# Attention outputs of six batches a layer as seven products added to the residual stream, tokens filled in batch by batch, and statistics of the last layer one a stage

## The chip, the core and the metric

The kernel runs on one core of a Trainium2 chip. Its engines are TensorE (PE, with weight loads as PEld), VectorE (DVE), ScalarE (ACT), GpSimd (POOL) and SyncE (SP), which issues most DMAs. Each works through its own queue in order and waits on semaphores for the others. The metric is the device time of one execution in microseconds (us), a median over runs. All data is float32.

## The reference

Eight batches of 512 tokens of width 512 pass two layers; each has a cross attention to 120 context rows of the batch, and a feed-forward part. LN is a layer norm.

```python
x = x + tanh(g_xattn[0]) * L0_xattn(LN(x), ctx)          # 16 heads of 32
x = x + tanh(g_ffn[0])   * L0_ffn(LN(x))                 # routed in groups of 32 tokens
x = x + tanh(g_xattn[1]) * L1_xattn(LN(x), ctx, mask)    # with biases and a key mask
x = x + tanh(g_ffn[1])   * L1_ffn(LN(x))                 # mixes each token with the one before
# attention: q = x Wq', k = ctx Wk', v = ctx Wv'; out = softmax(q k' / sqrt(32)) v; return out Wo'
```

## The kernel before

The stream `x` stays in SBUF, 32 tiles of 128 tokens, four tiles a batch. `CrossAttention` first projects keys and values (`project_keys`, `project_values`), then runs one stage a tile (`run`, then `tail` for the last tiles). The order on PE is written out by hand in the source; in the loop `run` the order on DVE, ACT and POOL is a planner's and fixed in the built program.

Stage t works on several tiles at once: `scores(t + 1)` makes the scores s of the next tile and emits its softmax, `queries` makes a quarter of the query products of the next batch, `output(t - 1)` multiplies the attention result of the tile before with Wo, `transpose_probs(t)` transposes this tile's probabilities, `transpose_x` transposes a normalised tile of two batches on (xnps to xnT), `after(t, 1)` does routing products in layer 0 (rlps, rxps, pps), and `attend(t)` multiplies probabilities with values (aps, copied to aT). `output` is split: two of its four matmuls stand before `transpose_probs`, two behind; in every fourth stage it is three and one.

The softmax of a tile is, on DVE, a maximum of each half of s (mx, nmx), a subtraction in the first half (L527), a sum (L533) and reciprocals (L506); on ACT eight exponentials of the second half (L517) and one of the first (L528); on POOL a scaling of each half (L507). `transpose_probs` then writes tps, copied to prT by DVE (first half) and ACT (second half).

PSUM has two pools. `p_s` has two places, tag "s", taken in turn by the two halves of s and the two halves of tps (L474, L543). `p_mm` has four places, tag "mm", taken in turn by every other product.

`SevenProducts` computes a 512 x 512 x 512 product in seven quarter products (`p1` to `p7`, each four matmuls of 256 columns, `multiply`) where the plain way takes eight. It needs four sums of quarters on each side (`left_steps`, `right_steps`); queries, keys, gates and values of the last layer use it already. Their sums for queries are made on POOL.

In layer 0, `route_stats` takes a tile's layer norm statistics (DVE, then three small POOL steps, L58 to L61), and `route_norm` writes the tile aside by DMA and normalises it in place on ACT (L714). In layer 1, `stats` only measures; the tiles of the last two batches are measured in `ChannelMix.run`, inside its stages of seven products.

## Time and profile before

| | us |
|---|---|
| median of 3 runs | 1442.75 (1442.69 to 1443.22) |
| profiled execution, own time | 1441.8 |
| its span | 1440.0 |
| layer 0 attention, one batch in the loop | 49.6 |
| layer 1 attention, one batch in the loop | 44.4 |
| PE busy in the span | 1386.5 |
| output products (L598), 512 records | 239.6 busy, 594 ns each |

The span is that of the instructions in the trace; the execution's own time is 1.8 us more. A matmul in float32 shows as two records, a transpose as one; records overlap, so a group's pace is read from starts: eight records of L598, one tile, take 3.44 us start to start, eight of L149 (one of the seven products) 1.72. In a time-ordered view a row has start, length, engine, line, operation, output<-input, and count of merged records; in brackets stands the idle time before it and what ended it. In a view by stretches the columns are length and the busy time of PE, PEld, DVE, ACT, POOL, then granted clock, DMA share and GB/s.

### The profile page before, as it was taken

The page shows a single profiled execution, that of the slowest core. Times are in us where ns is not written, and L with a number is a line of the kernel's source. Part 1 is how long each engine was busy: PE and PEld are TensorE (multiplying, and loading weights), DVE is VectorE, ACT ScalarE, POOL GpSimd, SP SyncE. Part 2 cuts the span into 40 slices and gives each one's busy share as a digit, 9 for nine tenths or more (in the row PEclk, how much of TensorE's full clock was granted, in tenths as well). Part 3 has the DMA queues.
Part 4 walks back from the last instruction along what each step waited for, and adds up shares of the span by engine and source line. Part 5 has one row for each costly group of instructions (what it writes and reads, how often), then busy time and mean ns, then how long its engine had stood idle before and what let it go on. Part 6 is the DMA issues. An engine that isn't in the chain of part 4 may idle for free.

```text
span 1440.0 us, 32567 instructions
## 1 busy us (share of the span) xinstructions
PE 1386.5 (96%) x13728; PEld 1067.2 (74%) x13728; DVE 1022.6 (71%) x1457; ACT 770.6 (54%) x1874; POOL 643.4 (45%) x576
## 2 busy tenths in 40 slices
PE   7999999999999997999999999999998999999997
PEld 3477777777776787888657777777775888888886
DVE  2767767777777776777576777777777677777786
ACT  1246666666666445444225665666566644445543
POOL 0425545545543001555375665666547233343331
PEclk9999999999999999999999999999999999999999
DMA  9200000000001347433301000000000000000001
GB/s 301 104 9 23 24 23 23 24 21 18 24 30 46 126 134 228 120 105 86 117 0 60 2 2 2 1 2 2 2 30 2 1 30 30 30 30 30 30 16 44
DMA packets 44886, 69.46 MB, mean 48 GB/s; under 512 B 2891, under 2 KB 20811, under 8 KB 44739
## 3 DMA queue, kind: packets, MB, share of 16 engines
q1 hardware_dynamic: 44451, 67.37, 14.5%
q8 instruction: 108, 1.77, 0.5%
q14 instruction: 39, 0.32, 0.1%
q10 hardware_dynamic: 288, 0.00, 0.0%
HBM read 50.59 MB, written 16.78 MB: 47 GB/s over the span
## 4 chain that ended last, share of the span: by engine, by line
PE 71%; DVE 15%; ACT 6%; POOL 4%; issue 3%; DMA 1%; POOLq 0%; DVEq 0%; ACTq 0%
PE ops L598 14%; PE qps L149 13%; PE tps L546 6%; PE cps L149 5%; PE aps L581 4%; PE s L489 4%; PE kps L342 4%; PE rps L992 3%; PE vps L361 3%; PE rlps L731 2%; PE l1ps L907 2%; PE ops L1013 2%; DVE rT L972 2%; PE xnps L421 2%; PE gps L880 2%
## 5 line engine op out<-in xcount | busy, mean ns | idle before, releaser
L507 POOL TENSOR_TENSOR pr<-pr,rs 128x960 f32<-128x960 f32 x128 | 229.0, 1792 | 250.6 <-DVE rs L506 229.2
L598 PE MATMUL ops<-wo,aT 128*128 128x512 f32 x512 | 239.6, 594 | 0.7 <-ACT aT L589 0.7
L517 ACT ACTIVATE pr<-s,nmx 128x120 f32<-128x120 f32 x512 | 176.7, 371 | 113.6 <-DVE nmx L514 105.5
L598 PEld LDWEIGHTS ops<-wo,aT 128*128 128x128 f32 x512 | 92.2, 190 | 71.9 <-issue 67.0
L1005 POOL TENSOR_TENSOR r<-r,b 128x1024 f32<-128x1024 f32 x31 | 73.5, 2378 | 144.3 <-ACT r L1004 144.3
L149 PE MATMUL qps<-xnT,wq 128*128 128x256 f32 x512 | 119.6, 381 | 0.0
L546 PEld LDWEIGHTS tps<-ident,pr 128*120 128x120 f32 x864 | 96.8, 138 | 29.5 <-issue 26.2
L525 DVE TENSOR_REDUCE mx<-s 128x8 f32<-128x960 f32 x64 | 73.9, 1155 | 56.7 <-PE s L489 56.7
L517 ACT ACTIVATION_READ_ACCUMULATOR pr<-s,nmx 128x1 f32 x512 | 111.1, 217 | 0.0
L546 PE MATMUL tps<-ident,pr 128*120 128x128 f32 x864 | 104.8, 273 | 2.5 <-ACT pr L517 1.3
L149 PEld LDWEIGHTS qps<-xnT,wq 128*128 128x128 f32 x512 | 95.7, 189 | 15.2 <-issue 1.0
L533 DVE TENSOR_REDUCE sm<-pr 128x8 f32<-128x960 f32 x64 | 73.5, 1149 | 22.1 <-ACT pr L528 22.0
L49 DVE BATCH_NORM_STATS2 bnst<-x 128x6 f32<-128x512 f32 x128 | 86.8, 678 | 1.3
L422 ACT COPY xnT<-xnps 128x512 f32<-128x512 f32 x64 | 38.0, 594 | 82.1 <-PE xnps L421 82.1
L514 DVE TENSOR_REDUCE nmx<-s 128x8 f32<-128x960 f32 x64 | 73.5, 1148 | 5.7 <-PE s L489 5.7
L581 PE MATMUL aps<-prT,v 120*32 120x128 f32 x2048 | 72.3, 276 | 4.7 <-ACT prT L571 2.7
L527 DVE TENSOR_TENSOR pr<-s,mx 128x960 f32<-128x960 f32 x64 | 73.5, 1149 | 0.9
L556 ACT COPY prT<-tps 120x1024 f32<-120x1024 f32 x54 | 55.0, 1018 | 32.6 <-PE tps L546 32.6
L1258 POOL TENSOR_TENSOR x<-x,cv 128x512 f32<-128x512 f32 x28 | 39.7, 1416 | 71.9 <-DVE cv L1255 71.9
L489 PE MATMUL s<-kT,qT 32*128 32x120 f32 x2048 | 71.1, 275 | 0.0
L489 PEld LDWEIGHTS s<-kT,qT 32*128 32x128 f32 x2048 | 65.6, 186 | 6.4 <-issue 6.3
L581 PEld LDWEIGHTS aps<-prT,v 120*32 120x32 f32 x2048 | 53.2, 109 | 18.7 <-issue 8.4
(189 smaller groups left out, 3101.7 us busy)
## 6 DMA issues: line engine op xcount, KB each, us to landing
w<-in_w_dram SPq DMA_DIRECT2D x32, 512.0 KB, 5.0
x<-in_x_dram SPq DMA_DIRECT2D x8, 1024.0 KB, 15.6
aside<-x SPq DMA_DIRECT2D x32, 256.0 KB, 2.0
x<-aside SPq DMA_DIRECT2D x8, 1024.0 KB, 10.2
out_dram<-x SPq DMA_DIRECT2D x14, 512.0 KB, 2.8
ctx<-in_ctx_dram SPq DMA_DIRECT2D x4, 960.0 KB, 11.7
wk<-in_wk_dram SPq DMA_DIRECT2D x3, 1024.0 KB, 11.2
wv<-in_wv_dram SPq DMA_DIRECT2D x3, 1024.0 KB, 6.2
```

The source lines that it names most:

```text
L49: cm.nc.vector.bn_stats(st, cm.x[:, t, :])
L149: self.nc.tensor.matmul(ps[:, m, :], self.a[a][:, k, m * P : (m + 1) * P], self.b[b][:, k, :], start=(k == 0), stop=(k == 1),)
L489: nc.tensor.matmul(s[j // 2][:, j % 2, hc * LK : (hc + 1) * LK], self.qT[b][r : r + 32, hc, toks], self.kT[r : r + 32, hc, keys], start=no ...
L507: nc.gpsimd.tensor_tensor(pr[:, js, :, :], pr[:, js, :, :], rs[:, js, :, :].to_broadcast([P, 2, NC, LK]), ALU.mult,)
L514: nc.vector.tensor_reduce(nmx, sv[1], AX.X, ALU.max, negate=True)
L517: nc.scalar.activation(pr[:, 2 + j, hc, :], sv[1][:, j, hc, :], AF.Exp, bias=nmx[:, j, hc, :], accum_out=sm[:, 2 + j, hc : hc + 1],)
L525: nc.vector.tensor_reduce(mx, sv[0], AX.X, ALU.max)
L527: nc.vector.tensor_tensor(pv, sv[0], mx.to_broadcast([P, 2, NC, LK]), ALU.subtract)
L533: nc.vector.tensor_reduce(sm[:, :2, :], pv, AX.X, ALU.add)
L546: nc.tensor.transpose(ps[:, jj, hc * P : (hc + 1) * P], pr[:, 2 * u + jj, hc, :], self.cm.ident,)
L581: nc.tensor.matmul(aps[32 * j : 32 * j + 32, hc, :], self.v[b // 2][:LK, b % 2, h * HD : (h + 1) * HD], prT[:, j, hc, :], start=True, stop ...
L598: nc.tensor.matmul(ops, self.aT[t][:, c, :], self.wo[:, c, :], start=(c == 0), stop=(c == NC - 1),)
```

## The change

In both layers the outputs of batches 0 to 5 are made by seven products a batch (`SevenAdded`) from aT of four tiles and Wo, in place of four `output` calls. Products are added to `x` with the gate as they come: on DVE from PSUM, and for a sum shared by several quarters (t) through ACT or DVE and then POOL. Wo's four sums are made once a layer on POOL (`wos`), aT's four once a batch on DVE. aT becomes one buffer of four tiles, xnT one buffer; their sums lie in buffers of the coming queries. Tiles of x are now transposed, and queries made, batch by batch: in the last stage of a batch three transposes and two output products, in the first stage of the next one transpose and four output products, then one output product and seven query products in the two stages after. Batches 6 and 7 keep `output`, unsplit. Routing follows two tiles later and catches up in two late stages. In `ChannelMix` two tiles a stage are normalised and transposed, in two stages each; of the last two batches, one tile is measured in each stage of values and keys. The core of the diff:

```diff
@@ -110,7 +110,7 @@
             step(t3, b22, b12, ALU.subtract),
             step(t1, b12, b11, ALU.subtract),
             step(t2, b22, t1, ALU.subtract),
-            step(t4, t2, b21, ALU.subtract),
+            step(t4, *((b21, t2) if negated else (t2, b21)), ALU.subtract),
         ]
 @@ -204,6 +204,51 @@
         self.finish(0, 1, c12)
+class SevenAdded(SevenProducts):
+    def __init__(self, nc, psum, a, b, c, t, gate, order):
+        super().__init__(nc, psum, a, b, c, None, order=order)
+        self.t, self.gate = t, gate
+    def add(self, c, ps):
+        self.nc.vector.scalar_tensor_tensor(c, ps, self.gate, c, ALU.mult, ALU.add)
+    def add_sum(self, *places):
+        for c in places:
+            self.nc.gpsimd.tensor_tensor(c, c, self.t, ALU.add)
+    def p1(self):
+        ps = self.multiply("A11", "B11")
+        self.nc.scalar.activation(self.t, ps, AF.Copy, scale=self.gate)
+        self.add_sum(self.c[0, 0])
+    def p2(self):
+        self.add(self.c[0, 0], self.multiply("A12", "B21"))
+    def p5(self):
+        ps = self.multiply("S1", "T1")
+        self.add(self.c[0, 1], ps)
+        self.add(self.c[1, 1], ps)
+    def p6(self):
+        self.add(self.t, self.multiply("S2", "T2"))
+        self.add_sum(self.c[0, 1])
+    def p7(self):
+        self.add(self.t, self.multiply("S3", "T3"))
+        self.add_sum(self.c[1, 0], self.c[1, 1])
+    def p3(self):
+        self.add(self.c[0, 1], self.multiply("S4", "B22"))
+    def p4(self):
+        self.add(self.c[1, 0], self.multiply("A22", "T4"))
@@ -255,6 +299,10 @@
                 for b in (1, 2):
                     self.stats_of_batch(b)
             self.work = pool("at_work", 2)
+            sums = self.work.tile([P, 4, 2, 256], FP, name="wos", tag="xnT")
+            self.wos = [sums[:, i] for i in range(4)]
+            self.xnT = self.work.tile([P, NC, S + 1], FP, name="xnT")[:, :, :S]
+            self.aT = self.work.tile([P, NC, S], FP, name="aT", bufs=1)
             self.prologue()
...
@@ -377,17 +425,27 @@
         for b in range(3):
             self.project_values(b)
-        for t in range(2 * TB):
+        for t in range(TB):
             self.transpose_x(t)
             self.normalize(t + 2)
             if t < TB - 1:
                 self.project_values(t + 3)
-            elif t < 2 * TB - 1:
-                self.queries(0, t + 1 - TB)
-        rest = self.scores(0)
-        for b in range(B - 2, B):
-            self.project_values(b)
+        self.start_queries(0)
+        self.queries(4)
+        self.project_values(B - 2)
+        self.queries(2)
+        self.project_values(B - 1)
+        self.queries(1)
+        rest = None
+        for t in range(TB, 2 * TB):
+            self.transpose_x(t)
+            if t + 2 < 2 * TB:
+                self.normalize(t + 2)
+            if t == TB:
+                rest = self.scores(0)
         rest()
+        self.start_queries(1)
+        self.sum_output_weights()
...
@@ -432,35 +485,47 @@
             step()
         self.wq7 = SevenProducts.left(w, *sums)
+    def sum_output_weights(self):
+        w, sums = self.wo, self.wos
+        for step in SevenProducts.right_steps(w, *sums, self.nc.gpsimd, negated=True):
+            step()
+        self.wo7 = SevenProducts.right(w, *sums)
+    def quarters_of_queries(self, b):
+        if b not in self.qT:
+            self.qT[b] = self.work.tile([P, NC, S], FP, name="qT")
+        return {(i, j): quarter(self.qT[b], i, j) for i in (0, 1) for j in (0, 1)}
+    def bank(self):
+        return self.p_mm.tile([P, 2, 256], FP, name="qps", tag="mm")
     def start_queries(self, b):
-        xnT = self.xnT[b][:, :, :S]
-        own = self.work.tile([P, 2, 256], FP, name="xns", bufs=1)
-        sums = [quarter(xnT, 0, 1), quarter(xnT, 0, 0), own, quarter(xnT, 1, 0)]
-        engine = self.nc.gpsimd if b > 1 else self.nc.vector
+        nc, xnT = self.nc, self.xnT
+        c = self.quarters_of_queries(b)
+        sums = [quarter(xnT, 0, 1), quarter(xnT, 0, 0), c[1, 0], quarter(xnT, 1, 0)]
+        engine = nc.gpsimd if b > 1 else nc.vector
         steps = SevenProducts.right_steps(xnT, *sums, engine)
         for step in steps[:2]:
             step()
         self.later_sums = steps[2:]
-        self.xn7 = SevenProducts.right(xnT, *sums)
-    def queries(self, b, f):
...
+        self.q7 = SevenProducts(
+            nc, self.bank, self.wq7, SevenProducts.right(xnT, *sums), c,
+            lambda: quarter(xnT, 0, 1),
+            bias=(self.bqk[:, 0, 0:2], self.bmore) if self.biased else None,
+        )
+    def queries(self, n):
+        for _ in range(n):
+            self.q7.next()
+            if self.later_sums:
+                self.later_sums.pop(0)()
     def scores(self, t):
@@ -585,28 +650,41 @@
                     start=True,
                     stop=True,
                 )
-        self.aT[t] = self.work.tile([P, NC, P], FP, name="aT")
-        nc.scalar.copy(self.aT[t], aps)
-    def output(self, t, chunks):
-        nc, x = self.nc, self.cm.x
-        if 0 in chunks:
-            self.ops[t] = self.p_mm.tile([P, D], FP, name="ops", tag="mm")
-        ops = self.ops[t]
-        for c in chunks:
+        nc.scalar.copy(self.aT_of(t), aps)
+    def aT_of(self, t):
+        i = t % TB
+        return self.aT[:, :, i * P : (i + 1) * P]
+    def output(self, t):
+        nc, x, aT = self.nc, self.cm.x, self.aT_of(t)
+        ops = self.p_mm.tile([P, D], FP, name="ops", tag="mm")
+        for c in range(NC):
             nc.tensor.matmul(
-                ops,
-                self.aT[t][:, c, :],
-                self.wo[:, c, :],
-                start=(c == 0),
-                stop=(c == NC - 1),
+                ops, aT[:, c, :], self.wo[:, c, :], start=(c == 0), stop=(c == NC - 1)
             )
...
+        nc.vector.scalar_tensor_tensor(
+            x[:, t, :], ops, self.gate, x[:, t, :], ALU.mult, ALU.add
+        )
+    def start_outputs(self, b):
+        nc, aT = self.nc, self.aT
+        x = self.cm.x[:, b * TB : (b + 1) * TB, :]
+        c = self.quarters_of_queries(b + 2)
+        sums = [quarter(aT, 0, 1), c[0, 0], c[1, 1], c[0, 1]]
+        self.output_sums = SevenProducts.left_steps(aT, *sums, nc.vector)
+        self.o7 = SevenAdded(
+            nc, self.bank, SevenProducts.left(aT, *sums), self.wo7,
+            {(i, j): quarter(x, i, j) for i in (0, 1) for j in (0, 1)}, c[1, 0], self.gate,
+            "1256734",
+        )
     def after(self, t, stage):
@@ -616,31 +694,55 @@
     def run(self):
-        for t in range(-1, NT - TB - 1):
-            if t >= 0:
-                if t + 10 < NT:
-                    self.normalize(t + 10)
-                self.scores(t + 1)()
-            self.queries(*divmod(t + TB + 1, TB))
+        self.after(-1, 1)
+        for t in range(NT - TB - 1):
+            b, i = divmod(t, TB)
+            if i in (1, 2) and b + 2 < B:
+                self.normalize(TB * (b + 2) + i - 1)
+            if i == 1 and b > 0:
+                self.o7.next()
+            self.scores(t + 1)()
+            if i == 0 and b > 0:
+                self.transpose_x(TB * (b + 1) + 3)
+            if i == 3:
+                self.start_outputs(b)
+                self.transpose_x(TB * (b + 2))
+                self.normalize(TB * (b + 2) + 2)
+                self.o7.next()
+                self.transpose_x(TB * (b + 2) + 1)
+                self.normalize(TB * (b + 2) + 3)
+            elif i == 0 and b > 0:
+                self.o7.next(2)
+            elif b > 0 or i < 2:
+                self.queries(2)
             self.after(t, 0)
-            short = t % TB == TB - 2
-            ahead = 3 if short else 2
-            if t > 0:
-                self.output(t - 1, range(ahead))
-            x_ahead = short and not self.masked
-            if x_ahead and t + 9 < NT:
-                self.transpose_x(t + 9)
-            if t >= 0:
-                self.transpose_probs(t)
-            if t > 0:
-                self.output(t - 1, range(ahead, NC))
-            if t + 9 < NT and not x_ahead:
-                self.transpose_x(t + 9)
+            if t - 1 >= NT - 2 * TB:
+                self.output(t - 1)
+            self.transpose_probs(t)
+            if i == 3:
+                self.transpose_x(TB * (b + 2) + 2)
+            elif i == 0:
+                if b > 0:
+                    self.o7.next(2)
+                else:
+                    self.queries(1)
+            elif i == 2:
+                self.queries(2)
+            elif b > 0:
+                self.queries(1)
             self.after(t, 1)
-            if t >= 0:
-                self.attend(t)
+            self.attend(t)
+            if i == 3:
+                for step in self.output_sums:
+                    step()
+                self.o7.next()
+            elif i == 0 and b > 0:
+                self.start_queries(b + 1)
             self.after(t, 2)
     def tail(self):
@@ -753,25 +857,41 @@
             ALU.is_equal,
         )
+    @staticmethod
+    def tiles_ended(s):
+        if s < 24:
+            return [s - 4] if s >= 4 else []
+        return {24: [20, 21], 25: [22, 23, 24]}.get(s, [s - 1])
     def in_slot(self, s, attention, stage):
         last = NT - TB - 1
-        if stage == 2 and 0 <= s - 1:
-            self.route_stats(s - 1)
-        if (stage == 2 and (0 <= s - 1 < last - 1 or s == NT)) or (stage == 3 and s > last):
-            self.route_norm(s - 1 if stage == 2 else s - 2)
-        if stage != (0 if s == NT else 1):
-            return
-        pool = attention.p_mm
+        if stage == 2:
+            for t in self.tiles_ended(s):
+                self.route_stats(t)
+                if t < last - 1 or s == NT:
+                    self.route_norm(t)
+        if stage == 3 and s > last:
+            self.route_norm(s - 2)
         if s == -1:
             self.start()
-        if 0 <= s - 4:
-            self.route_logits(s - 4, pool.tile([P, D], FP, name="rlps", tag="mm"))
-        if 0 <= s - 3:
-            self.route_x(s - 3, pool.tile([P, D], FP, name="rxps", tag="mm"))
-        b = (s - 9) // TB
-        if (s - 9) % TB == 0 and 0 <= b < B - 2:
-            self.route_back(b, pool.tile([P, D], FP, name="pps", tag="mm"))
+        def bank(name):
+            return attention.p_mm.tile([P, D], FP, name=name, tag="mm")
+        if stage == (0 if s == NT else 1) or (stage == 0 and s in (last - 2, last - 1)):
+            t = self.t
+            if 0 <= t - 1:
+                self.route_logits(t - 1, bank("rlps"))
+            if 0 <= t:
+                self.route_x(t, bank("rxps"))
+            self.t += 1
+        if stage == (0 if s == NT else 1):
+            b = 5 if s == 29 else (s - 11) // TB
+            if s == 29 or ((s - 11) % TB == 0 and 0 <= b < B - 3):
+                self.route_back(b, bank("pps"))
...
@@ -1332,10 +1463,9 @@
                 work += sums(b + 1, 1)
             if b + 2 < B:
                 work += calls(self.normalize, *[(TB * (b + 2) + i,) for i in range(TB)])
+            work = self.turns(work)
             if b < TB:
-                t = NT - 2 * TB + 2 * b
-                work += calls(self.at.stats, *[(t + i,) for i in range(2)])
+                work[4].insert(0, lambda t=late + 2 * b: self.at.stats(t))
             self.stage(self.values(b), work)
```

## Prediction

> **What bounds it now.** I read the busy shares first, then the busy time by stretches of one batch, then the time-ordered TensorE rows of a stage with and without output products.
>
> ```profile
> PE 1386.5 (96%) x13728; PEld 1067.2 (74%) x13728; DVE 1022.6 (71%) x1457; ACT 770.6 (54%) x1874; POOL 643.4 (45%) x576
> 264.00:313.60 49.60, 49.60 (x481) 38.18 (x477) 35.42 (x57) 33.23 (x96) 25.34 (x26) 1.00 0.06 23
> 887.50:932.00 44.50, 44.50 (x445) 32.86 (x442) 32.90 (x47) 27.38 (x87) 27.83 (x23) 1.00 0.01 1
> ```
>
> The columns of the stretches are length, then PE, PEld, DVE, ACT, POOL busy. In both attention layers PE is busy all of a batch's 49.6 or 44.4 us, so a removed matmul pays in full only while everything feeding PE stays in time. How much time it has is seen in two stages of layer 0, a usual one and the first (t=0), which has no output products:
>
> ```profile
> 286.55 1.17 PE L489 MATMUL s<-kT,qT 32*128 32x120 f32 x32
> 287.65 1.99 PE L149 MATMUL qps<-xnT,wqs 128*128 128x256 f32 x8
> 289.48 1.89 PE L149 MATMUL qps<-xnT,wq 128*128 128x256 f32 x8
> 291.21 1.88 PE L598 MATMUL ops<-wo,aT 128*128 128x512 f32 x4
> 292.92 1.91 PE L546 MATMUL tps<-ident,pr 128*120 128x128 f32 x16
> ```
>
> ```profile
> 93.86 1.17 PE L489 MATMUL s<-kT,qT 32*128 32x120 f32 x32
> 94.96 1.99 PE L149 MATMUL qps<-xnT,wqs 128*128 128x256 f32 x8
> 96.79 1.89 PE L149 MATMUL qps<-xnT,wq 128*128 128x256 f32 x8
> 99.23 1.06 PE L546 MATMUL tps<-ident,pr 128*120 128x128 f32 x8 [0.56 <-DVE pr L527]
> 100.97 1.09 PE L546 MATMUL tps<-ident,pr 128*120 128x128 f32 x8 [0.67 <-ACT pr L517]
> ```
>
> Scores and probability transposes take turns in the same two PSUM places: tps of tile t overwrites s of tile t+1, its first half once DVE has subtracted the maximum (L527), its second once the eight exponentials (L517) have read. In the usual stage PE has two query products (3.56 us) and half an output (1.72) between s and tps. At t=0 only the queries stand there, and PE stalls.
>
> ```profile
> 287.75 1.16 DVE L525 TENSOR_REDUCE mx<-s 128x8 f32<-128x960 f32 x1 [1.26 <-PE s L489]
> 290.01 0.36 ACT L517 ACTIVATE pr<-s,nmx 128x120 f32<-128x120 f32 x1 [1.66 <-DVE nmx L514]
> 292.71 1.04 ACT L528 ACTIVATE pr<-pr 128x960 f32<-128x960 f32 x1
> ```
>
> From the end of s (287.65) the subtraction ends after 3.4 us (three 1.07 us steps) and the exponentials after 5.06. The second half of tps came at 292.92+0.87: 1.1 us to spare. That spare is the quantity to watch.
>
> **Products.** A 512-column matmul is two records, 0.86 us (3.44 a tile, 13.75 a batch); a 256-column one 0.43, so seven products are 28 x 0.43 = 12.03. Saved: 1.72 a batch, 20.6 for twelve. Everything else on PE is only moved.
>
> **What stands before tps now.** By the order of the changed program, between s and tps: last stage of a batch (call it 3): transpose, product, transpose = 2.7 us; stage 0: transpose and two products = 4.1; stages 1 and 2: two products = 3.56. All under the 4.2 (5.06 less tps's own first half, 0.87) that the second half needs. I walk layer 0 from the end of stage 3's s, each engine in its static order.
>
> Stage 3: tps starts 3.4, second half 5.06, ends 5.9 instead of 4.5. ACT then runs the pv exponential (to 6.05), the new scaled copy, an xnT copy and a normalisation before prT's second half (8.65); the next xnT copy, whose bank attend needs, ends 9.15. Attend ends 10.2, against 7.85 without waits: stall 2.35. Layer 1 has no routing work to cover this: attend would end at 5.97 and ends at 9.65 (third matmul waits for prT): 3.7.
>
> PE then does product 2 (to 11.95) and s (13.05). Stage 0: the four new sums need the last aT copy (10.85); DVE does them and product 2's add before the next maximum. At 0.69 each they end 14.2, while s was ready at 13.05. Subtraction 17.4, exponentials 19.1; PE reached tps at 17.1. Stall 1.2; layer 1, where the sums meet POOL work, 1.75.
>
> Stage 1: after tps (20.0) come products 7 and 3, routing, attend (25.9), product 4 (27.6) and s (28.7). DVE owes seven adds a batch (0.74 each, the four old STTs gone), two output adds and the stats, and starts the maximum 1.1 us late. Layer 1: o4 ends 26.4, s 27.6; DVE adds o4, takes two stats and aggregates (to 28.7), then maximum, negated maximum, subtraction to 31.9; exponentials end 33.6, 6.0 after s where two products and half of tps cover 4.4: stall 1.6. In layer 0 four of L714's normalisations stand together on ACT ahead of these exponentials. They wait for POOL: after the last x additions (26.9) come two query sums (1.1 each, to 29.2), then four chains, each 0.22+0.57+0.27 us from rows L58, L59, L61 and gaps, 5.0 in all: 34.2. The aside DMAs (2.0 us) are done by then. Last normalisation 35.0, q1's copy 35.5, exponentials 38.2, where s ended at 28.7: stall 5.1. Queued behind are q1's copy, DVE's add of it, and PE.
>
> Stage 2: DVE is punctual again, 5.06 against 4.4: 0.7.
>
> Sums: layer 0 9.4 - 1.7 = +7.7 a batch; layer 1 7.75 - 1.7 = +6.0. The sixth window keeps outputs of batch 6 between s and tps in stages 1 and 2 (+3.44), which hides 3.4 + 0.7 = 4.1 of waits in layer 0 and 1.6 + 0.7 = 2.3 in layer 1. So 6 x 7.7 - 4.1 = **+42**, 6 x 6.0 - 2.3 = **+34**.
>
> **First batch.** s(1) follows s(0) with only transposes between, so waits for s(0)'s readers (4.1 stall). Stage 0: batch 1's sums between DVE's maximum steps (row: one such sum took 1.70 before the maximum at t=0), 1.7. Stage 1: 0.7, and attend directly after tps 1.1. Stage 2: nothing before tps, 4.2. That is 11.8 against 4.0 before in layer 0 and about 2 in layer 1: **+18**.
>
> **Other costs.** POOL gets four 1.2 us additions a batch (25.3 + 4.8 = 30 of 57 us busy) and wos (four of 1.27): POOL waits elsewhere, 0; without that cover each would push a probability scaling by 1.2. The copy with the gate equals L161's 0.57 on ACT, counted above. Layer 1's stats in mix.run: gates of four batches stall 1.0 and some 0.3 more behind kT's last add; later batches (no stats) don't. Between 0 and -5.3; I take **-2**, since DVE's total before that add is unchanged. Route tiles two stages later, caught up in two late stages, and the paired mix transposes: PE work conserved, that tail had 4.1 us of waits, bound -3 to +3, 0.
>
> **A rule against a row.** The Trainium skill's "TensorE: Matmul & The Clock Gate" (Part 1) says that an idle window of about 3.4 us halves PE's clock for another. In this trace 1.41 us is the longest mid-run wait I found, with clock 1.00; but after the first 9.35 us the 16 ctps took 3.44 against 1.81 later. By the row of short waits, 0. By the rule five 5.1 us and two 4.2 us stalls would contain a whole window about half the time: 7 x 0.5 x 1.63 = 5.7, an estimate; I take **+4**, ends 0 and 11.
> "GPSIMD Engine Reference" (specifications) says two-input SBUF work on DVE contends with POOL. L107 on DVE took 0.69 where alone, 1.44 at the worst form's mean. Four sums at 0.69 are 2.8 us, contended 5.7. POOL mostly waits then: I take the first; the end is 3 x 12 = 36 more.
>
> **Sum.** 42 + 34 + 18 - 2 + 4 = +96. The profiled execution was 1441.8 (span 1440.0), 0.95 under the median: 1441.8 + 96 = **1538**.
>
> **Rivals.**
> Floor (25%): DVE punctual, ACT not blocked by normalisations. Then stalls are 2.35/3.7, 0.05, 0.7, 0.7, layer 0 +2.1, layer 1 +3.4 a batch: 6 x 5.5 - 2.8 + 18 = +48: 1490. For it: the static order is a planner's, and the statistics may become ready sooner than I walk. Against: t=0's trace shows a DVE sum delaying tps directly.
> Contention (11%): sums at the contended price, clock halved: +96 + 36 = 1574. Against: POOL is mostly waiting at those moments.
> Gain (3%): tps does not wait, saving all of 20.6: 1421. It decides where exponentials end within 4.4 us of s, below 5.06; nothing in the trace does so. Against it: t=0's two waits.
> Losses just cancelling the gain: 1%. Not doing what it says: the order shows 28 matmuls a batch in place of 16, so no chance of its own.
> Main, 60%, own range 1515 to 1560.
>
> **Range.** 1488 to 1566 takes in floor and main, leaving most of contention and gain out. A measurement tells 0.2% (3 us) from no change. Faster 0.03, same 0.01, slower 0.96.
>
> **What would show it.** PE idle before tps released by the exponentials and the subtraction in every stage; in layer 0 largest at stage 1, ending just after four normalisations; batch stretches of about 57 and 50 us; PE busy 20 us less. Wrong if PE stays full in these stretches, or if the exponentials end within 4.4 us of s.

## The result, and the profile after

| | before | after |
|---|---|---|
| median | 1442.72 us (1438.88 to 1443.22) | 1581.62 us (1577.82 to 1585.01) |
| profiled execution, own time | 1441.8 | 1585.0 |
| its span | 1440.0 | 1583.2 |
| mean granted clock of PE | 0.998 | 0.974 |

The ratio is 1.0964, with a 95% interval of 1.0943 to 1.0986: the change costs 139 us. Slower was forecast, 1538 us, with a range to 1566; the measured time lies 15.6 us beyond the upper end.

First the busy shares after the change, then the view by stretches: one batch of layer 0, one of layer 1, and the sixth and last such window of layer 0.

```profile
PE 1421.3 (90%) x14016; PEld 1144.2 (72%) x14016; DVE 1094.4 (69%) x1541; ACT 778.7 (49%) x1886; POOL 720.9 (46%) x632
248.70:309.10 60.40, 52.06 (x504) 44.20 (x500) 40.99 (x64) 33.62 (x96) 30.07 (x30) 0.94 0.05 19
943.30:998.00 54.70, 46.40 (x472) 38.05 (x472) 39.15 (x53) 28.21 (x88) 33.91 (x26) 0.97 0.00 1
429.56:492.83 63.27, 58.85 (x544) 48.16 (x540) 45.26 (x76) 34.58 (x98) 32.18 (x36) 1.00 0.07 26
```

Three things are to be seen. A batch takes 60.4 and 54.7 us in place of 49.6 and 44.4, where about 57 and 50 had been forecast. PE is no longer full: it idles 8.3 us in each of the two batches. And PE is busy 35 us *more* over the whole run, although 20.6 us of matmuls were taken out, while the clock column fell to 0.94 and 0.97. The second fact is the mechanism of the forecast; the third is what it missed.

The view of PE's waits names the mechanism. Before, no row of tps in it came to more than 1.4 us in total; now two such rows are at the top. The columns are the total, the count and the longest.

```profile
PE tps L611 <- ACT pr L582: 51.5, 48, 4.5
PE tps L611 <- DVE pr L592: 34.5, 32, 3.5
PE aps L646 <- ACT prT L621: 13.9, 10, 1.7
```

L582 and L592 are the exponentials and the subtraction (L517 and L527 before), L611 the transposes of the probabilities. So tps does wait for the readers of the next tile's scores, in nearly every stage. The worst stage is the one forecast, stage 1 of layer 0. Here it is in time order on PE:

```profile
277.91 1.17 PE L554 MATMUL s<-kT,qT 32*128 32x120 f32 x32
279.00 3.72 PE L149 MATMUL qps<-xnT,wq 128*128 128x256 f32 x16
283.76 1.06 PE L611 MATMUL tps<-ident,pr 128*120 128x128 f32 x8 [1.03 <-POOL rstd L59]
288.24 1.96 PE L611 MATMUL tps<-ident,pr 128*120 128x128 f32 x8 [3.42 <-ACT pr L582]
289.99 3.48 PE L149 MATMUL qps<-xnT,wqs 128*128 128x256 f32 x8
```

and on ACT, where four normalisations of the routed layer (L818, L714 before) wait for POOL's chains and stand ahead of the exponentials; the last two are these, with a query copy and the first exponential behind them:

```profile
283.26 1.70 ACT L818 ACTIVATE x<-x,nmr,rstd 128x512 f32<-128x512 f32 x2 [0.71 <-POOL nmr L61]
284.86 0.56 ACT L161 COPY qT<-qps 128x512 f32<-128x512 f32 x1
285.33 0.36 ACT L582 ACTIVATE pr<-s,nmx 128x120 f32<-128x120 f32 x1
```

The reader should now compare lengths on PE. Behind the wait, eight transposes take 1.96 us and one product 3.48, where the other stages show 1.09 and 1.89. PE runs at half clock there. The view by stretches says so directly. Taken for PE alone, its columns are length, PE busy, granted clock, DMA share and GB/s:

```profile
282.96:286.37 3.41, 1.06 (x8) 1.00 0.00 0
286.37:289.78 3.41, 1.54 (x7) 0.50 0.02 5
289.78:293.20 3.42, 3.42 (x10) 0.50 0.00 0
```

(The 1.03 us before the first half of tps are put down to POOL's rstd, which tps does not read; the subtraction L592 ended then, at 283.61.) Stage 0 of layer 1 shows the same with shorter waits:

```profile
959.70 1.89 PE L149 MATMUL qps<-wos,qT 128*128 128x256 f32 x8
963.40 1.06 PE L611 MATMUL tps<-ident,pr 128*120 128x128 f32 x8 [1.81 <-DVE pr L592]
965.26 1.65 PE L611 MATMUL tps<-ident,pr 128*120 128x128 f32 x8 [0.79 <-ACT pr L582]
966.70 3.05 PE L149 MATMUL qps<-wos,qT 128*128 128x256 f32 x8
969.59 1.89 PE L149 MATMUL qps<-wo,qT 128*128 128x256 f32 x8
```

```profile
962.22:965.63 3.41, 1.43 (x11) 1.00 0.01 2
965.63:969.04 3.41, 3.41 (x13) 0.50 0.00 0
```

DVE's subtraction is late there because its sums of aT (L88) stand before the maximum and run beside POOL's additions of the output bias:

```profile
955.09 0.88 DVE L88 TENSOR_TENSOR qT<-aT 128x512 f32<-128x512 f32 x1 [3.04 <-ACT aT L653]
956.01 1.64 DVE L88 TENSOR_TENSOR aT<-aT 128x512 f32<-128x512 f32 x1
...
958.23 1.10 DVE L88 TENSOR_TENSOR qT<-aT 128x512 f32<-128x512 f32 x1
959.37 0.69 DVE L88 TENSOR_TENSOR qT<-aT,qT 128x512 f32<-128x512 f32 x1
```

```profile
955.39 3.40 POOL L468 TENSOR_TENSOR x<-x,gbo 128x512 f32<-128x512 f32 x2
```

**The whole account.** For both kernels I summed PE's rows of the two attention loops, from the first scores to the last. For each row, start to next start is the idle time in the brackets plus the time occupied. The occupied time was set against the pace of the undisturbed rows of before (eight records of L149 1.72 us, sixteen of tps 1.75, 32 of s 1.10, and so on).

| us | before | after | difference | forecast |
|---|---|---|---|---|
| PE idle in both loops | 2.5 + 5.6 | 57.9 + 61.3 | +111 | 42 + 34 + 18 + 20.6 = +115 |
| rows slower than their pace | 5.7 + 6.0 | 32.9 + 34.3 | +55.5 | +4 |
| products saved | | | -20.6 | -20.6 |
| last layer's mix (trace, from the last scores on) | 337.6 | 332.8 | -4.8 | -2 |
| sum | | | +141 | +96 |

The span grew by 143.2; the 2 us left over were not traced to a place. Some work only changed sides: in each layer about 5.5 us (the values of two batches out of the loop, three transposes of x into it) now stand ahead of the loop, and the sum leaves them out. Of the 55.5 us, 31.9 (17.1 and 14.8) lie in rows that took over 1.35 times their usual pace, half-clock or "cold" rows; before has none. The other 24 lie in small pieces at the waits: in the rows above, the product before a wait occupies 1.89 instead of 1.72, and tps cut in two by a wait 1.06 and 0.93 instead of 1.75. With some 100 waits of tps and aps in the list, that is about a quarter of a microsecond each beside the idle time shown. Much of it is overlap: a product's row is 1.89 long with a wait behind it or without, but without one the next row starts about 0.16 before its end (966.70 + 3.05 is 969.75, and the next row starts at 969.59). The trace models the ends of matmuls, so the idle time in brackets, counted from such an end, is less than what a wait costs.

**When the clock falls.** In the two loops the granted clock is halved sixteen times, each time for 3.41 or 6.83 us, 75 us in all; PE is busy for 66.7 of them, and half of that, 33, is near the 31.9 of the rows. All these stretches start on one grid of 3.413 us: in stage 1 of layer 0 at 166.91, 228.35, 286.37, 347.81 and 409.25, that is 18, 17, 18 and 18 such steps apart. The whole trace was laid on this grid, leaving out its first 20 us and its end, and PE's busy time was taken in each window that had full clock. All 15 windows with under 1.55 us of busy time were followed by half clock, none of the 407 with over 1.87, and 2 of the 11 between. Over all thirteen traces of this case it is 93 of 94, none of 5352, and 29 of 108. So idle time is added up within a window, and the edge lies near half of it.

### The profile page after: what moved, and what is told of

It is laid out like the page before. It is cut to its first block, busy times and chain, and to the rows that moved or that the text cites. A ratio compares the mean times of both kernels' runs of the same rounds, so it can differ in the third digit from the quotient of the medians.

```text
span 1583.2 us, 33359 instructions
## 1 busy us (share of the span) xinstructions
PE 1421.3 (90%) x14016; PEld 1144.2 (72%) x14016; DVE 1094.4 (69%) x1541; ACT 778.7 (49%) x1886; POOL 720.9 (46%) x632
## 4 chain that ended last, share of the span: by engine, by line
PE 52%; DVE 20%; ACT 18%; POOL 5%; issue 4%; DMA 1%; ACTq 0%; DVEq 0%; POOLq 0%
PE qps L149 14%; ACT pr L582 9%; PE cps L149 4%; PE tps L611 4%; PE aps L646 4%; PE kps L390 3%; PE ops L664 3%; PE rps L1112 3%; PE s L554 3%; PE vps L409 2%; DVE nmx L579 2%; DVE mx L590 2%; PE l1ps L1027 2%; PE ops L1133 2%; PE rlps L835 2%
## 5 line engine op out<-in xcount | busy, mean ns | idle before, releaser
L582 ACT ACTIVATE pr<-s,nmx 128x120 f32<-128x120 f32 x512 | 177.2, 373 | 64.4 <-DVE nmx L579 58.5
L611 PE MATMUL tps<-ident,pr 128*120 128x128 f32 x864 | 125.0, 293 | 91.2 <-ACT pr L582 51.5
L611 PEld LDWEIGHTS tps<-ident,pr 128*120 128x120 f32 x864 | 100.4, 146 | 119.2 <-ACT pr L582 63.6
L149 PE MATMUL qps<-xnT,wq 128*128 128x256 f32 x512 | 126.2, 396 | 0.0
L582 ACT ACTIVATION_READ_ACCUMULATOR pr<-s,nmx 128x1 f32 x512 | 111.6, 218 | 0.0
L149 PEld LDWEIGHTS qps<-xnT,wq 128*128 128x128 f32 x512 | 97.0, 196 | 16.1 <-issue 0.4
L222 POOL TENSOR_TENSOR x<-x,qT 128x512 f32<-128x512 f32 x48 | 60.7, 1276 | 82.8 <-DVE qT L218 82.8
L646 PE MATMUL aps<-prT,v 120*32 120x128 f32 x2048 | 76.6, 279 | 18.3 <-ACT prT L621 13.9
L619 DVE COPY prT<-tps 120x1024 f32<-120x1024 f32 x54 | 65.3, 1210 | 28.0 <-PE tps L611 27.9
L653 ACT COPY aT<-aps 128x512 f32<-128x512 f32 x64 | 38.0, 594 | 81.5 <-PE aps L646 81.5
L554 PE MATMUL s<-kT,qT 32*128 32x120 f32 x2048 | 74.5, 282 | 2.7 <-DVE pr L592 2.6
L592 DVE TENSOR_TENSOR pr<-s,mx 128x960 f32<-128x960 f32 x64 | 73.6, 1150 | 0.8
```

What stands on the lines that cost most here:

```text
L149: self.nc.tensor.matmul(ps[:, m, :], self.a[a][:, k, m * P : (m + 1) * P], self.b[b][:, k, :], start=(k == 0), stop=(k == 1),)
L554: nc.tensor.matmul(s[j // 2][:, j % 2, hc * LK : (hc + 1) * LK], self.qT[b][r : r + 32, hc, toks], self.kT[r : r + 32, hc, keys], start=no ...
L582: nc.scalar.activation(pr[:, 2 + j, hc, :], sv[1][:, j, hc, :], AF.Exp, bias=nmx[:, j, hc, :], accum_out=sm[:, 2 + j, hc : hc + 1],)
L592: nc.vector.tensor_tensor(pv, sv[0], mx.to_broadcast([P, 2, NC, LK]), ALU.subtract)
L611: nc.tensor.transpose(ps[:, jj, hc * P : (hc + 1) * P], pr[:, 2 * u + jj, hc, :], self.cm.ident,)
L646: nc.tensor.matmul(aps[32 * j : 32 * j + 32, hc, :], self.v[b // 2][:LK, b % 2, h * HD : (h + 1) * HD], prT[:, j, hc, :], start=True, stop ...
```

## Experiments

Eleven kernels were run, each timed beside the kernel before. The theory: cover on PE between s and tps is too short, tps waits for the readers of the scores, and the waits cost PE its clock. The rivals: the sums, additions and normalisations on the other engines set the pace, whatever the order; or PE's slow rows have another cause.

| kernel | median us | range | ratio to before, 95% |
|---|---|---|---|
| plain_out | 1492.92 | 1489.63 to 1494.44 | 1.0359 [1.0340, 1.0379] |
| no_norm | 1551.47 | 1547.38 to 1555.43 | 1.0769 [1.0742, 1.0795] |
| no_sums | 1552.86 | 1550.58 to 1557.32 | 1.0782 [1.0760, 1.0805] |
| no_gbo | 1567.68 | 1566.54 to 1572.91 | 1.0872 [1.0842, 1.0902] |
| warm | 1566.79 | 1564.67 to 1569.82 | 1.0878 [1.0854, 1.0901] |
| warm2 | 1566.31 | 1565.52 to 1574.12 | 1.0877 [1.0847, 1.0906] |
| warm3 | 1562.96 | 1561.16 to 1567.67 | 1.0837 [1.0807, 1.0868] |
| three_ahead | 1552.17 | 1549.68 to 1555.66 | 1.0763 [1.0743, 1.0783] |
| ahead_bare | 1473.17 | 1470.66 to 1474.91 | 1.0214 [1.0186, 1.0242] |
| tps_mm | 1556.53 | 1555.72 to 1558.98 | 1.0794 [1.0777, 1.0812] |
| mix_alone | 1438.33 | 1436.16 to 1439.70 | 0.9972 [0.9959, 0.9986] |

### More cover: the outputs by plain products before tps

```diff
-            if i == 1 and b > 0:
-                self.o7.next()
...
-            elif b > 0 or i < 2:
+            elif i > 0 and b > 0 or b == 0 and i < 2:
                 self.queries(2)
             self.after(t, 0)
-            if t - 1 >= NT - 2 * TB:
+            if t > 0:
                 self.output(t - 1)
             self.transpose_probs(t)
```

> The changed kernel with its order of tokens by batches, its query products and its route stages, but the outputs made by four 512-column matmuls a tile, as before, and all four placed between a tile's scores and the transposes of its probabilities (t); no sums of aT, no additions on POOL, no copy with the gate. PE then has 13.75 us of output matmuls a batch in place of 12.03, 1.72 more. Theory (what stands between s and tps on PE decides; with 3.44 us more before every tps the cover is at least 7 us against the 4.2 that the second half needs): the waits of PE for the exponentials and the subtraction nearly vanish in the late batches, only the first batch's stalls stay (about 18 us and cold matmuls), and the mix part keeps its gain of about 5: about 1475, 1465 to 1490. Rival (the batch-wise order itself, with its normalisations on ACT and the route stages two stages later, costs): the stall of layer 0's second stage stays at 5 us a batch and the time is 1520 or more.

1492.9 us, 89 less than the changed kernel, with 20.6 us more of matmuls. The two totals of tps (51.5 and 34.5) fall: the one for the exponentials to 3.7, the other to 0.8. A batch takes 51.7 us in layer 0 (53.4 where the clock was halved once) and 47.8 in layer 1, with 1.8 and 2.9 us of waits. So the waits come with the change of the outputs and leave with it; the order by batches alone costs no 5 us in stage 1. As this kernel also does without the sums of aT, POOL's additions and the copy with the gate, it does not show the cover by itself (the other order further down does). It still costs 50 us over before, more than expected: new waits of attend for DVE's copy of tps (20.5 us) and of the outputs for the copy of aT (12.7), and the first batch.

### The normalisations ahead of the exponentials

```diff
-        nc.scalar.activation(
-            x, x, AF.Identity, bias=self.cm.nmr[:, t, :], scale=self.cm.rstd[:, t, :]
-        )
+        if t >= 24:
+            nc.scalar.activation(
+                x, x, AF.Identity, bias=self.cm.nmr[:, t, :], scale=self.cm.rstd[:, t, :]
+            )
```

> The changed kernel without the ACT normalisations of the routed layer (L818) for tiles 0 to 23, so the routing sees x before its normalisation; everything else is issued as before. Theory (in layer 0's stage 1 the exponentials stand on ACT behind four such normalisations that wait for POOL's chains, 3.4 us of wait, and PE is cold afterwards, some 2.5 us): stage 1 falls from 17.8 to about 12, 6 us x 6 batches = -36, about 1546. Rival (the wait is caused by the number of products before tps alone, ACT is late for another reason): stage 1 keeps its wait and the time stays within 10 us of 1581.6. In both, layer 1 stays at 54.7 us a batch.

1551.5, 30 less, where 36 was expected. In three of the six batches stage 1 fell to 12.72 us, start of s to start of s, from 16.9 to 18.3; the wait of 3.42 became 0.72. That ACT stood behind L818 is thereby shown, as the cause of the longest wait. Two of the other batches had half clock once (13.5 and 14.4 us), and the sixth also does output tiles: with the same two waits of 1.03 and 0.72, one batch runs at full clock and the next does not. These are PE's rows of two such stages, one batch apart, and the windows of the grid around them:

```profile
273.36 1.06 PE L611 MATMUL tps<-ident,pr 128*120 128x128 f32 x8 [1.03 <-POOL rstd L59]
275.14 1.09 PE L611 MATMUL tps<-ident,pr 128*120 128x128 f32 x8 [0.72 <-ACT pr L582]
276.06 1.89 PE L149 MATMUL qps<-xnT,wqs 128*128 128x256 f32 x8
...
328.66 1.06 PE L611 MATMUL tps<-ident,pr 128*120 128x128 f32 x8 [1.03 <-POOL rstd L59]
330.44 1.49 PE L611 MATMUL tps<-ident,pr 128*120 128x128 f32 x8 [0.72 <-ACT pr L582]
331.72 3.21 PE L149 MATMUL qps<-xnT,wqs 128*128 128x256 f32 x8
```

```profile
269.54:272.95 3.41, 2.79 (x13) 1.00 0.35 131
272.95:276.37 3.42, 2.29 (x18) 1.00 0.00 0
...
327.57:330.98 3.41, 1.66 (x14) 1.00 0.00 0
330.98:334.39 3.41, 3.41 (x13) 0.50 0.02 5
```

In the first batch the two waits are spread over two windows, in the second they fall into one. The expectation was wrong about layer 1, which was to stay at 54.7 us a batch. By the profiled executions layer 0's loop gave 25.5 us and layer 1's, which the edit does not touch, 11.5: there stage 0 kept its two waits, 1.84 and 0.72 to 1.00, in all batches but the last, and its clock in all of them (one such window had 1.57 us of busy time, where the changed kernel's had 1.43). So part of the 30 is the luck of where waits fall on the grid.

### The sums of aT on DVE, and what slows them

```diff
-            nc, self.bank, SevenProducts.left(aT, *sums), self.wo7,
+            nc, self.bank, SevenProducts.left(aT, *[quarter(aT, 0, 1)] * 4), self.wo7,
...
-                for step in self.output_sums:
-                    step()
                 self.o7.next()
```

> The changed kernel without the four sums of aT on DVE that each batch of outputs needs (the products S1 to S4 take a quarter of aT in their place, so these outputs are not the reference's). Theory (the sums stand on DVE before the next tile's maximum and are slowed by POOL's additions in layer 1): layer 1's stage 0 starts its maximum 2.4 us earlier, the wait for the subtraction goes and PE stays warm, -24 over six batches; layer 0's stage 0 loses its 1.2 us, -7: about 1550. If the sums only fill time in which DVE would wait anyway: 1575 to 1582. With the wait gone but the clock still halved in layer 1's stage 0: about 1565.

1552.9, 28.8 less, and stage 0 of layer 1 fell from 18.06 to 13.99 us: the first of the three cases. The sums are on the path. The next run leaves the sums and takes away what runs beside them:

```diff
-        if self.biased:
+        if self.biased and t < 2 * TB:
             nc.gpsimd.tensor_tensor(cm.x[:, t, :], cm.x[:, t, :], self.gbo, ALU.add)
```

> The changed kernel without POOL's addition of the output bias (L468) to the tiles of batches 2 to 7 in layer 1, so that these tiles lack that bias. DVE's order stays as it is. In the changed kernel the four sums of aT in layer 1's stage 0 take 0.88, 1.64, 1.10 and 0.69 beside two such additions. Theory (the additions slow the sums, and the late maximum makes tps wait and halves the clock): the sums return to about 2.8 in all, 1.4 a batch goes with the wait, -8, and where the clock then stays whole another -11: 1562 to 1574. If the sums take that long of themselves or for another reason: within 4 of 1581.6.

1567.7, in the middle of the theory's range. DVE's order is the same and the sums are back at their length:

```profile
955.40 0.69 DVE L88 TENSOR_TENSOR aT<-aT 128x512 f32<-128x512 f32 x1
...
956.67 0.68 DVE L88 TENSOR_TENSOR qT<-aT 128x512 f32<-128x512 f32 x1
957.39 0.69 DVE L88 TENSOR_TENSOR qT<-aT,qT 128x512 f32<-128x512 f32 x1
```

0.69 where it was 1.64, 0.68 where it was 1.10. The wait for the subtraction fell from 1.81 to 0.47, and the half clock behind it went as well: a batch takes 51.6 us, 3.1 less, of which 1.34 is that wait and 1.7 the clock.

### The clock: work that nothing uses, put into the waits

```diff
+            if i == 1 and b > 0 and not self.masked:
+                ps = self.p_mm.tile([P, D], FP, name="warm", tag="mm")
+                for c in range(NC):
+                    self.nc.tensor.matmul(
+                        ps, self.wo[:, c, :P], self.wo[:, c, :], start=(c == 0), stop=(c == NC - 1)
+                    )
             self.after(t, 0)
```

> The changed kernel with four more matmuls of 512 columns (3.44 us at full clock) between the query products and the transposes of the probabilities in layer 0's second stage of batches 1 to 6; their result is used nowhere. That fills the wait of 1.0 + 3.4 us there with work. Theory (the eight transposes at 1.96 in place of 1.09 and the eight query matmuls at 3.48 in place of 1.89 behind that wait run at half clock because PE stood still): they return to about 1.1 and 1.9, the wait falls from 4.4 to about 1, and the time falls by 2.5 x 6 = 15 to about 1567, although PE does more. Rival (the rows behind the wait are slow for another reason, such as their input or a bank): they stay slow and the time is the same or some us longer.

```profile
276.98 3.60 PE L726 MATMUL warm<-wo 128*128 128x512 f32 x8
280.41 1.04 PE L611 MATMUL tps<-ident,pr 128*120 128x128 f32 x8
282.63 1.09 PE L611 MATMUL tps<-ident,pr 128*120 128x128 f32 x8 [1.19 <-ACT pr L582]
283.56 1.89 PE L149 MATMUL qps<-xnT,wqs 128*128 128x256 f32 x8
```

The inputs of these rows come no earlier than before, PE does 3.4 us more, and the rows behind the wait are back at 1.09 and 1.89. A stage takes 15.40 in place of 17.83, and the kernel is faster. Half clock in layer 0's loop falls from 41.0 to 13.7 us. So the slow rows are the clock, and idleness makes it. The total, 14.8 less, matches the expected 15 partly by chance: by the trace, layer 0's loop gives 8.9 of it (cold rows 17.1 to 7.7), as the sixth window was not cold before and pays for the fill, and the half clock there had been shorter in some batches.

The next run filled layer 1's stage 0 and the first batches too.

```diff
+    def fill(self, n):
+        if n:
+            ps = self.p_mm.tile([P, D], FP, name="warm", tag="mm")
+        for c in range(n):
+            self.nc.tensor.matmul(
+                ps, self.wo[:, c, :P], self.wo[:, c, :], start=(c == 0), stop=(c == n - 1)
+            )
...
+            if t == 0:
+                self.fill(3)
             self.scores(t + 1)()
...
+            if b > 0:
+                self.fill(0 if i > 1 else i * 4 * (not self.masked) or (1 - i) * 2 * self.masked)
+            elif i == 2:
+                self.fill(4)
             self.after(t, 0)
```

> The changed kernel with more matmuls that nothing uses, 512 columns each, wherever PE was seen to fall to half clock: four in layer 0's stage 1 (as in the run before), two before tps in layer 1's stage 0, and in the first batch of both layers three before the second tile's scores and four before the third tile's tps. Clock theory: beside the 15 of the four alone, layer 1's stage 0 gives 1.8 x 6 = 11 and the first batches about 4 each, 8: about 1581.6 - 34 = 1547, granted clock 0.99 or more. If the clock is not the cause there: 1565 to 1575, since the added matmuls only fill waits.

1566.3: a miss. The granted clock came out as forecast (0.992), but the time did not: the added matmuls come to some 43 us, and the idle time of both loops fell by only 32. Stage 0 of layer 1 did fall to 16.4, but the first three fills came to stand behind a transpose that waits 5.2 us for ACT's normalisation, behind the idle time instead of in it, and the first batches grew by 1.6 and 1.9. The same without the first batches' fills (the `t == 0` and `i == 2` lines left out):

> The changed kernel with unused matmuls of 512 columns in the loop only: four in layer 0's stage 1 (these alone gave 1566.8) and two before tps in layer 1's stage 0, nothing in the first batches. In the run that also filled the first batches, layer 1's stage 0 fell from 18.06 to 16.4 by its trace but the first batches grew, 10.5 us of new waits of xnps for ACT. Clock theory: 1566.8 - 1.7 x 6 = about 1556. If layer 1's stage 0 only seemed shorter: 1566.

1563.0, seven more than expected, between the two cases. Cold rows of layer 1's loop fell from 14.8 to 6.1 us, and stage 0 to 16.4; but in the run with the four alone, which the expectation started from, only four of the six stages had fallen to half clock, so 1.7 x 4 was there to gain. By the two profiles layer 1's loop gave 7.1. Single executions differ by a few us elsewhere (the part between the last scores of layer 0 and the first of layer 1 ranged from 317.7 to 326.8 us over the profiles with this order), so the clock's size is better read from the rows than from these medians.

### The same products in another order

```diff
-            if i == 1 and b > 0:
+            if i == 1 and b > 0 and not self.masked:
                 self.o7.next()
             self.scores(t + 1)()
+            if i == 1 and b > 0 and self.masked:
+                self.o7.next()
...
                 self.normalize(TB * (b + 2) + 3)
+                self.o7.next()
             elif i == 0 and b > 0:
-                self.o7.next(2)
+                self.o7.next(3)
             elif b > 0 or i < 2:
-                self.queries(2)
+                self.queries(3 if b > 0 and (i == 2 or not self.masked) else 2)
```

> The changed kernel with its products placed otherwise on PE, none added or left out: in the last stage of a batch two products of outputs in place of one stand between s and tps, in stage 0 three in place of two, in stage 2 three in place of two; in stage 1 of layer 0 three query products, in layer 1 the seventh product of outputs and two queries behind s. Cover before the second half of tps is then 5.3, 6.5, 6.0 and 6.0 us in place of 3.6, 5.0, 4.4 and 4.4, against the 5.06 that the exponentials need. Theory (this cover decides, and the clock follows from it): waits stay mainly in layer 0's stage 1 (4.45 less 1.72 = 2.7) and before attend in the last stages (1.7); batches of about 51.5 and 45.5 us in place of 60.45 and 54.7; 1581.6 - 6 x 9 - 6 x 9 = about 1473, 1455 to 1500. Rival (the sums, additions and normalisations on DVE, POOL and ACT set the pace of a batch): 1540 or more.

1552.2: far from 1473 and within the rival's forecast, so the cover alone is not enough. The view of waits says why; the two waits of tps have shrunk, and two new waits are at the top.

```profile
PE qps L149 <- POOL xnT L107: 25.1, 6, 4.2
PE qps L149 <- DVE aT L88: 14.2, 11, 2.2
...
PE tps L611 <- DVE pr L592: 7.4, 4, 3.5
PE tps L611 <- ACT pr L582: 5.6, 12, 0.9
```

The 86 us of waits of tps became 13, as the theory says; but the products moved forward now wait for their own sums, in layer 0 for the query sums that stand on POOL behind the four statistics chains (4.2 a batch), in layer 1 for DVE's sums of aT (2.2). The wait moved from one input to the next. The clock did not come back with the cover either: the loops have 85 us at half clock in place of 75, and each of the six batches of layer 0 with the 4.2 us wait has 6.83 of it. The last run takes these two inputs away, with this order:

```diff
-            nc, self.bank, SevenProducts.left(aT, *sums), self.wo7,
+            nc, self.bank, SevenProducts.left(aT, *[quarter(aT, 0, 1)] * 4), self.wo7,
...
-                for step in self.output_sums:
-                    step()
+                pass
...
             for t in self.tiles_ended(s):
+                if t < 24:
+                    self.nc.sync.dma_start(
+                        out=self.aside[t * P : (t + 1) * P, :], in_=self.cm.x[:, t, :]
+                    )
+                    continue
                 self.route_stats(t)
```

> The kernel with three products ahead of tps (1552), less what its trace shows in the place of the removed waits: without the four sums of aT a batch (the outputs take a quarter of aT instead) and, for tiles 0 to 23 of layer 0, without the statistics and the normalisation of the routed layer (so the routing sees x unnormalised). The products on PE stay all. Theory (behind the cover, what bounds is the work that the change moved in front of the products: POOL's statistics chains ahead of the query sums, 4.2 us a batch, and DVE's sums of aT, 0.6 and 2.2 a batch, with the clock that these waits cost, some 3): layer 0 falls from 58.1 to about 49.5 a batch, layer 1 from 50.3 to about 46.5, so 1552 - 52 - 22 = about 1478, 1465 to 1500. Rival (other parts of the batch-wise order, the exponentials on ACT for instance, set 50 us or more a batch anyway): 1525 or more.

1473.2. A batch takes 49.9 and 45.2 to 46.8 us, with 1.2 and 1.9 to 2.2 of waits; the expected sum held. The cover alone gave 29 us and both together 108, so both constraints, the cover and the work around the products, make the loss. Taking that work away in the old order was run only in parts (no_sums 29, no_norm 30), not in one kernel; and this kernel also does less than it must, so some of its gain is work left out. Even this bare kernel is not under before: its first batches still wait, and it does not reach 47.9 and 42.7 us a batch.

### Transposes in the other pool

```diff
-        for u in range(2):
-            ps = self.p_s.tile([LK, 2, NC * P], FP, name="tps", tag="s")
...
+        for j in range(4):
+            ps = self.p_mm.tile([LK, NC, P], FP, name="tps", tag="mm")
+            for hc in range(NC):
+                nc.tensor.transpose(ps[:, hc, :], pr[:, j, hc, :], self.cm.ident)
+            if j < 2:
+                nc.vector.tensor_copy(prT[:, j, :, :], ps)
             else:
-                nc.scalar.copy(dst, src)
+                nc.scalar.copy(prT[:, j, :, :], ps)
```

> The changed kernel with the transposes of the probabilities in four places of the other PSUM pool (p_mm), so that they no longer overwrite the scores of the next tile; two of the four are copied by DVE and two by ACT. Theory (the shared place makes tps wait): the waits of tps for the exponentials and the subtraction go, 86 us in the changed kernel. What remains is the copy of tps, which stands on ACT and DVE behind the same exponentials and makes attend, one product later, wait, so that only the 0.9 to 1.8 us of the transposes come out of each late stage: 24 stages of each layer by about 1.2, and some of the clock: 1500 to 1545. Rival (the wait is the queue on ACT alone, the place does not matter): the same total, 1575 to 1590, all of it now before attend.

1556.5, between the two forecasts, so a miss of the theory. The waits of tps for the exponentials and the subtraction are gone from the list, so the shared place made them; in their stead tps and the products wait for places of the one pool to be read out (tps for DVE's x 16.7 us and for ACT's qT 10.6, xnps for ACT's qT 17.3, products for ACT's qT 6.9). It does not tell the rest of the two theories apart.

### The mix part alone

```diff
+                turns = self.turns(chunks(b, 0) + sums(b, 0))
+                if b <= TB:
+                    turns[1].insert(0, lambda t=late + 2 * b - 1: self.at.stats(t))
...
-                work += calls(self.at.stats, *[(t + i,) for i in range(2)])
+                work[4].insert(0, lambda t=late + 2 * b: self.at.stats(t))
```

> The kernel before, with one part of the change alone: in the last layer's mix the tiles of the last two batches are measured one a stage, in the stages of values and of keys, in place of two at the end of the values. My forecast's term was -2 with bounds 0 and -5.3. By the trace of the changed kernel, where the four batches with statistics take 38.75 us in place of 40.03 and the waits of PE for kT's last add (four of 1.0) go: -4.9, about 1437 where before is 1442. If that gain belongs to the other parts of the change (more of DVE's time free at that point): 0 to -2. In the first case this beats both kernels.

The view of waits, of before and then of this kernel:

```profile
PE cps L149 <- DVE kT L203: 4.0, 4, 1.0
```

```profile
PE cps L149 <- DVE kT L203: 0.4, 1, 0.4
```

1438.33 beside 1442.35 on the same chip, 4.0 us less, and by the interval faster than before, by 0.3%. This part of the change is worth keeping without the rest; it is the only kernel that beats both.

## Why the prediction was right or wrong

Right: the sign, the mechanism and its place. "tps of tile t overwrites s of tile t+1", so saved matmuls turn into waits. The four stalls of a batch, forecast and measured as idle time on PE: in layer 0 2.35, 1.2, 5.1, 0.7 against 1.77, 1.23, 4.45, 0.88; in layer 1 3.7, 1.75, 1.6, 0.7 against 3.15, 2.60, 1.67, 0.88. Over both loops the idle time grew by 111 us where the steps add up to 115. The first batches, up to the scores of the fifth tile, idled 9.5 and 10.4 us where 11.8 was walked, against 2.5 and 1.5 before where 4.0 and 2 had been taken.

Wrong: the clock term. The prediction set the rule of a 3.4 us idle window in the Trainium skill ("TensorE: Matmul & The Clock Gate", Part 1) against rows of short waits, and took "+4, ends 0 and 11". Measured: 32 us of half-clock rows. The step that failed is its premise: "five 5.1 us and two 4.2 us stalls would contain a whole window about half the time". It counted only the longest stalls and gave each a half chance, since a whole window had to be idle. In the trace, a window in which PE was busy less than about half was enough. Layer 1's stage 0, which the estimate left out, loses its clock after 1.81 and 0.79 us of waiting with 1.06 us of transposes between, in five batches of six, and in the run without normalisations 1.03 and 0.72 were enough once. So a window need not be wholly idle; here the measurement decides against the rule as I read it. The same section says the window is free-running; the grid of 3.413 us agrees with that, as waits shift against it from batch to batch. The row that I set against the rule ("1.41 us is the longest mid-run wait I found, with clock 1.00") was of waits that stood alone; it said nothing of several within one window, which is what the change makes.

Wrong too: "Everything else on PE is only moved." It is moved, but cut by waits, and each wait costs about a quarter of a us beyond the idle time shown, 24 us in sum; the walk charged only the idle time. With the half clock it is why PE, forecast to be busy 20 us less, was busy 35 us more. These two terms, 28 us more for the clock and 24 for the cuts, less the 4 us too much of idle time and the 3 too little for the mix, account for 45 of the 47 us by which the profiled execution (1585.0) missed its sum (1537.8).

Mis-sized but small: DVE's sums of aT in layer 1. "At 0.69 each" held in the run without POOL's additions (but for the first, 0.91) and not in the changed kernel (0.88, 1.64, 1.10, 0.69), so stage 0's idle time was 2.60 for 1.75. The Trainium skill's rule on two-input work on DVE beside POOL ("GPSIMD Engine Reference", specifications), weighed against the row, was right here; "POOL mostly waits then" was not. The gain of the mix was at the far end of its bounds, 4.8 (the run of it alone: 4.0) for 2, because the full 1.0 wait of each of four batches left. "The sixth window keeps outputs of batch 6 between s and tps": in layer 0 it idled 4.4 us where the other batches idle 8.3, so 3.9 were hidden for the 4.1 walked.

Rivals: the floor (1490) fell because ACT was blocked by the normalisations, as feared; contention (1574) was nearest in time and partly its cause, the clock above all. The range failed because the clock's upper end, 11, was an estimate from a rule on whole windows, and because the cuts had no term at all.

Open: what decides in a window with 1.55 to 1.87 us of busy time, and what the cuts cost beside the lost overlap. Spreading the statistics chains so that they do not stand before the query sums was not tried.

## What to carry to other kernels

Before shortening the work of a full engine, ask what that work was covering: here four output matmuls a tile hid the 5 us between scores and the release of their PSUM places, and taking out 1.7 us a batch cost over 10. When a walk shows waits on PE close together, price them at their idle time plus a cut each; and where they leave PE busy for less than about half of some 3.4 us, add a half-clock stretch, 1.7 to 2.5 us here, and do not wait for one long gap. And when a change has several parts, price and run them apart: the small part that nobody would have named first was the one worth 4 us.

## What was unexpected of the hardware

The clock of PE fell after 2.6 us of idle time in two pieces, 2.0 of them in one window of the 3.41 us grid, and in one case after 1.75, all in one window. Adding 3.4 us of useless matmuls to each of six stages made layer 0's loop 8.9 us shorter (435.7 to 426.8). And the same two waits in neighbouring batches once cost clock and once did not, so that such a loss differs from batch to batch in one execution, and from one kernel to another in a layer that the edit did not touch: layer 1's loop took 406.9 us in the changed kernel and 395.3 without layer 0's normalisations.
